# A linear attention and its token normalisation, computed another way in a four-layer hybrid kernel

## The chip, the core and the metric

The kernel runs on one core of one Trainium2 chip. The metric is the time on the device in microseconds (us). Three runs of the kernel before gave 10989.94, 10992.03 and 10992.92 us; the median is 10992.03. One more run was profiled: its span is 10992.0 us.

The core has five engines with a queue each, which run side by side and wait for one another through semaphores: TensorE (PE in the profile, with its weight loads as PEld), VectorE (DVE), ScalarE (ACT), GpSimd (POOL) and SyncE (SP), which issues the DMAs.

## The reference

The input is four images of 64 x 64 tokens with 96 channels. Layers 0 and 1 are selective scans (a state-space layer in four directions); they are not concerned here. Layers 2 and 3 work on the tokens `t`, 4096 per image:

```
t = t + attn(_ln_t(t), Wqkv, bqkv, Wff, bff)
t = t + ffn(_ln_t(t), W1, b1, W2, b2)

_ln_t(v):  (v - mean(v)) / sqrt(var(v) + 1e-5)          over the 96 channels of a token

attn(x):   qkv = x @ Wqkv + bqkv;  q, k, v = split(qkv, 3), 6 heads of 16
           attn = einsum('bhnd,bhmd->bhnm', q, k) * D ** (-0.5)
           y = einsum('bhnm,bhmd->bhnd', attn, v)         # no softmax
           return y @ Wff + bff

ffn(x):    h = relu(_qlinear(x, W1, b1));  return _qlinear(h, W2, b2)
           # _qlinear: inputs and weights rounded to an 8-bit float (5 exponent bits,
           # 2 mantissa bits), results to a 16-bit float
```

There is no softmax, so the two products of the attention can be taken in either order: first `k` transposed times `v`, a 96 x 96 matrix per image, and then the queries times that.

## The kernel before, in words

The scan layers take up the first part of the program. Their results lie in DRAM; four tiles `tok[b]` of 128 x 32 x 96 (partition, token tile, channel) are then loaded, one per image, and stay in SBUF to the end. For each of the layers 2 and 3 the kernel runs `attention` and then `ffn`. Each of the two opens its own pools of tiles and closes them at its end, and loops over the four images.

`token_norm` serves both. Per image it goes over 32 tiles of 128 tokens. On VectorE it takes a statistic (`bn_stats`, L685) and an aggregate (`bn_aggr`, L686) of each tile. `rstd_of` then adds epsilon on VectorE (`tn_ve`, L79) and raises the 128 x 32 variances to the power -0.5 on GpSimd (`tn_rs`, L81). The tiles are normalised into `tn` (L691), three of four on VectorE and the fourth on GpSimd. Groups of four tiles are turned by the PE (L695, channels to the partitions) and evicted by ScalarE (L696), into `tnt` in the attention, and as 8-bit floats into `xq` in the feed-forward.

`attention` then does, per image:

- the queries, 8 products of 512 tokens (L724), evicted by ScalarE into `qt` (L725). `tnt` and `qt` have a 97th row of ones, set by GpSimd (L717, L720), which carries the bias;
- keys and values, 32 products of 128 tokens (L732), evicted in pairs by VectorE into `kv` (L734), and summed over all tokens in `vk` (L736) on the PE;
- `vk` cut to its heads (L745), multiplied with `Wff` (L747) and copied to `wq` (L750), whose last row is the bias `bff`, loaded by DMA for each image (L749);
- the output, 32 products (L755), added to `tok` in groups of four tiles by VectorE (L757).

`ffn` does, per image, 8 chunks of 512 tokens. In each there are three products of 128 hidden channels (L793), cast to a 16-bit float by ScalarE (`h`, L795), bias and relu on VectorE (`hb`, L797), and a cast to an 8-bit float on GpSimd (`hq`, L798). The second product (L802) follows, its eviction on ScalarE (`o`, L806), its bias on VectorE (`ob`, L808) and the addition to `tok` (L810). Layer 3 writes each image out at its end (L812).

The order of the instructions on each engine is laid out when the program is built: an instruction that stands earlier in the program has precedence, and a later one is drawn forward where the layout finds a gap. On the chip each engine takes its queue in that order. Most tiles have two buffers, so the work on the next image can begin while one is under way. The products of 32-bit floats show as two PE records each, the transposes and the 8-bit products as one.

Of the kernel before, what the change touches and what calls it, by code (L numbers as in the profile page):

```python
# [16 lines left out]
F32 = mybir.dt.float32  # L17
# [3 lines left out]
AF = mybir.ActivationFunctionType  # L21
ALU = mybir.AluOpType
# [5 lines left out]
L = HW * HW  # L28
C = 96
# [16 lines left out]
NT = L // 128  # L46
# [29 lines left out]
def rstd_of(nc, pool, var, shape, tag, half):  # L76

    ve = pool.tile(shape, F32, name=f"{tag}_ve")
    nc.vector.tensor_scalar(ve, var, EPS, None, ALU.add)  # L79
    rs = pool.tile(shape, F32, name=f"{tag}_rs")  # L80
    nc.gpsimd.tensor_tensor(rs, ve, half, ALU.pow)  # L81
    return rs
# [594 lines left out]
        finish_sum(len(steps) - 1)  # L677


def token_norm(nc, pool, pp, ident, half, t, out):  # L680

    stats = pool.tile([128, NT, 6], F32, name="tstats")
    mv = pool.tile([128, NT, 2], F32, name="tmv")
    for j in range(NT):
        nc.vector.bn_stats(stats[:, j], t[:, j])  # L685
        nc.vector.bn_aggr(mv[:, j], stats[:, j])  # L686
    rs = rstd_of(nc, pool, mv[:, :, 1], [128, NT], "tn", half)
    tn = pool.tile([128, NT, C], F32, name="tn")
    for j in range(NT):
        eng = nc.gpsimd if j % 4 == 3 else nc.vector  # L690
        eng.tensor_scalar(tn[:, j], t[:, j], mv[:, j, 0:1], rs[:, j : j + 1], ALU.subtract, ALU.mult)  # L691
    for g in range(NT // 4):
        ps = pp.tile([C, 512], F32, name="tnps", tag="tp")
        for j in range(4):
            nc.tensor.transpose(ps[:, 128 * j : 128 * j + 128], tn[:, 4 * g + j], ident)  # L695
        nc.scalar.activation(out[:C, 512 * g : 512 * g + 512], ps, AF.Copy, saturate=False)  # L696


def attention(tc, cst, ident, half, tok, w):

    nc = tc.nc
    with ExitStack() as stage:
        p1 = stage.enter_context(tc.tile_pool(name="t1", bufs=1))
        p2 = stage.enter_context(tc.tile_pool(name="t2", bufs=2))
        pp = stage.enter_context(tc.tile_pool(name="t_ps", bufs=2, space=PSUM))


        wqkv = p1.tile([C + 1, 3 * C], F32, name="wqkv")
        nc.sync.dma_start(out=wqkv[:C], in_=w["Wqkv"])
        nc.sync.dma_start(out=wqkv[C : C + 1], in_=w["bqkv"].unsqueeze(0))  # L710
        wff = p1.tile([C, C], F32, name="wff")
        nc.sync.dma_start(out=wff, in_=w["Wff"])

        for b in range(NB):
            t = tok[b]
            tnt = p2.tile([C + 1, L], F32, name="tnt")
            nc.gpsimd.memset(tnt[C : C + 1], 1.0)  # L717
            token_norm(nc, p2, pp, ident, half, t, tnt)
            qt = p2.tile([C + 1, L], F32, name="qt")
            nc.gpsimd.memset(qt[C : C + 1], 1.0)  # L720
            for c in range(L // 512):
                cols = slice(512 * c, 512 * c + 512)
                ps = pp.tile([C, 512], F32, name="qps", tag="mm")
                nc.tensor.matmul(ps, wqkv[:, :C], tnt[:, cols], start=True, stop=True)  # L724
                nc.scalar.copy(qt[:C, cols], ps)  # L725

            vk = pp.tile([C, C], F32, name="vk", tag="vk", bufs=1)
            for g in range(NT // 2):
                ps = pp.tile([128, 2, 2 * C], F32, name="kvps", tag="mm")
                for j in range(2):  # L730
                    at = 256 * g + 128 * j
                    nc.tensor.matmul(ps[:, j], tnt[:, at : at + 128], wqkv[:, C:], start=True, stop=True)  # L732
                kv = p2.tile([128, 2, 2 * C], F32, name="kv", bufs=3)
                nc.vector.tensor_copy(kv, ps)  # L734
                for j in range(2):
                    nc.tensor.matmul(  # L736
                        vk,
                        kv[:, j, C:],
                        kv[:, j, :C],
                        start=(g == 0 and j == 0),  # L740
                        stop=(g == NT // 2 - 1 and j == 1),
                    )

            heads = p2.tile([C, C], F32, name="heads")
            nc.vector.tensor_tensor(heads, cst["heads"], vk, ALU.mult)  # L745
            ps = pp.tile([C, C], F32, name="wps", tag="vk", bufs=1)
            nc.tensor.matmul(ps, heads, wff, start=True, stop=True)  # L747
            wq = p2.tile([C + 1, C], F32, name="wq")
            nc.sync.dma_start(out=wq[C : C + 1], in_=w["bff"].unsqueeze(0))  # L749
            nc.vector.tensor_copy(wq[:C], ps)  # L750
            for g in range(NT // 4):
                po = pp.tile([128, 4, C], F32, name="ops", tag="o")
                for j in range(4):
                    at = 512 * g + 128 * j
                    nc.tensor.matmul(po[:, j], qt[:, at : at + 128], wq, start=True, stop=True)  # L755
                tg = t[:, 4 * g : 4 * g + 4]
                nc.vector.tensor_tensor(tg, tg, po, ALU.add)  # L757


def ffn(tc, ident, half, tok, w, out=None):  # L760

    nc = tc.nc
    NH = HID // 128
    with ExitStack() as stage:
        p1 = stage.enter_context(tc.tile_pool(name="f1", bufs=1))
        p2 = stage.enter_context(tc.tile_pool(name="f2", bufs=2))
        pp = stage.enter_context(tc.tile_pool(name="f_ps", bufs=2, space=PSUM))
# [15 lines left out]

        for b in range(NB):
            t = tok[b]
            xq = p2.tile([C, L], E5M2, name="xq")
            token_norm(nc, p2, pp, ident, half, t, xq)
            for c in range(L // 512):
                cols = slice(512 * c, 512 * c + 512)
                hq = p2.tile([128, NH, 512], E5M2, name="hq")  # L790
# [25 lines left out]
def hybrid_kernel(ctx: ExitStack, tc: tile.TileContext, a):  # L816
    nc = tc.nc
# [7 lines left out]
    cst = {}  # L825
# [31 lines left out]
    tok = []  # L857
# [1 line left out]
        tok.append(ptok.tile([128, NT, C], F32, name=f"tok{b}"))  # L859
        nc.sync.dma_start(out=tok[b], in_=x[b * L : (b + 1) * L, :].rearrange("(p j) c -> p j c", j=NT))  # L860
    for n in (2, 3):
        attention(tc, cst, ident, half, tok, {k: a[f"l{n}_{k}"] for k in ("Wqkv", "bqkv", "Wff", "bff")})
        ffn(tc, ident, half, tok, {k: a[f"l{n}_{k}"] for k in ("W1", "b1", "W2", "b2")}, a["out"] if n == 3 else None)


# [77 lines left out]
def kernel_arrays(inputs):  # L943
    import numpy as np

    arrays = {"x": np.asarray(inputs["x"]).reshape(NB * L, C), **constants()}
    arrays |= scan_weights(inputs, 0, "out_norm_w") | scan_weights(inputs, 1, "out_norm_g")
    for n in (2, 3):
        for name in ("Wqkv", "bqkv", "Wff", "bff"):
            arrays[f"l{n}_{name}"] = np.asarray(inputs[f"L{n}_attn_{name}"])  # L950
        arrays[f"l{n}_W1"] = np.asarray(inputs[f"L{n}_ffn_W1"]).T
        arrays[f"l{n}_b1"] = np.asarray(inputs[f"L{n}_ffn_b1"]).reshape(HID // 128, 128).T
        arrays[f"l{n}_W2"] = np.asarray(inputs[f"L{n}_ffn_W2"]).T
        arrays[f"l{n}_b2"] = np.asarray(inputs[f"L{n}_ffn_b2"])
    return {name: np.ascontiguousarray(v) for name, v in arrays.items()}
# [16 lines left out]
```

## Time and profile before

| What | us |
|---|---|
| Median of three runs | 10992.03 |
| Span of the profiled run | 10992.0 |
| Scan layers, to the loading of the tokens | 0 to 10262.3 |
| Layer 2, attention | 10262.3 to 10455.5 |
| Layer 2, feed-forward | 10455.5 to 10622.4 |
| Layer 3, attention | 10622.4 to 10818 |
| Layer 3, feed-forward | 10818 to 10992 |

The busy shares over the whole span are PE 75%, VectorE 90%, ScalarE 79% and GpSimd 83%, but most of the span belongs to the scans. A row of the groups gives the line, the engine, the operation, output and inputs by the names of the program, shapes and count; behind the bar stand the busy time and the mean duration of one instruction, and then the idle time of the engine before these instructions with what ended it. A row of the timeline gives the start, the length, the engine, the line and the operation, "xN" for N merged instructions, and in brackets the idle time before it.

### The profile page before, as it was taken

How to read it: one execution, taken by the hardware profiler on the slowest of the kernel's cores; microseconds unless marked ns; L12 is line 12 of the kernel's file. 1: busy time of each engine (PE TensorE's matmuls, PEld its weight loads, DVE VectorE, ACT ScalarE, POOL GpSimd, SP SyncE). 2: the span in 40 equal slices, each digit the busy share in tenths (PEclk: the TensorE clock that was granted, in tenths of full speed). 3: DMA queues.
4: the chain of work that ended last, by engine and by line, in shares of the span. 5: the costliest groups of instructions: out<-in, count | busy, mean ns of one | idle time of the engine just before them, and what ended most of it. 6: DMA issues, size and time to landing. Idle time of an engine off the chain costs nothing. (4 is left out here: it accounts for less than half of the span.)

```text
span 10992.0 us, 145011 instructions
## 1 busy us (share of the span) xinstructions
PE 8224.2 (75%) x48624; PEld 6063.9 (55%) x48624; DVE 9903.3 (90%) x7866; ACT 8663.0 (79%) x18359; POOL 9100.6 (83%) x5250
## 2 busy tenths in 40 slices
PE   7777777777777777777777777776877777776767
PEld 4555555554555555555555555555555555555645
DVE  7999999996999999998899999998899999998576
ACT  6888888885888888885888888886688888887233
POOL 3999999992999999994799999996599999998364
PEclk9889999988889899988888989998888999998767
DMA  4677777774677777776567777777577777777200
GB/s 126 204 206 219 218 220 220 218 213 135 205 212 215 213 218 219 213 218 163 180 208 211 215 218 220 219 214 194 153 206 210 216 219 218 218 216 202 75 3 25
DMA packets 960110, 2114.22 MB, mean 192 GB/s; under 512 B 413154, under 2 KB 704292, under 8 KB 761636
## 3 DMA queue, kind: packets, MB, share of 16 engines
q1 hardware_dynamic: 959364, 2104.94, 66.7%
q8 instruction: 386, 6.32, 0.2%
q14 instruction: 360, 2.95, 0.1%
HBM read 1943.20 MB, written 161.48 MB: 191 GB/s over the span
## 5 line engine op out<-in xcount | busy, mean ns | idle before, releaser
L71 POOL TENSOR_TENSOR h<-h,cb 128x1024 f32<-128x1024 f32 x3072 | 7198.5, 2366 | 271.5 <-issue 83.6
L71 DVE TENSOR_TENSOR_SCAN h<-da,last,bp 128x1024 f32<-128x1024 f32 x2064 | 4735.4, 2335 | 129.7 <-PE bp L71 12.4
L71 ACT ACTIVATE x<-dut,bt 128x128 f32<-128x128 f32 x12288 | 3495.0, 370 | 1.2 <-PE bp L71 0.6
L71 PE MATMUL yp<-ident,h 128*128 128x128 f32 x24576 | 3325.6, 295 | 9.8 <-POOL h L71 9.8
L71 PEld LDWEIGHTS yp<-ident,h 128*128 128x128 f32 x24576 | 3151.7, 155 | 126.9 <-issue 76.3
L71 ACT ACTIVATE da<-delta,amat 128x1024 f32<-128x1024 f32 x2752 | 3063.9, 1138 | 181.9 <-DVE h L71 181.3
L71 PE MATMUL bp<-ident,x 128*128 128x128 f32 x10240 | 1651.6, 313 | 1308.7 <-DVE h L71 902.4
L71 PEld LDWEIGHTS bp<-ident,x 128*128 128x128 f32 x10240 | 1333.6, 160 | 1872.3 <-ACT x L71 1035.2
L71 DVE TENSOR_TENSOR bp<-du,bp 128x1024 f32<-128x1024 f32 x1472 | 1779.8, 1213 | 240.5 <-PE bp L71 238.4
L71 DVE TENSOR_TENSOR_SCAN h<-da,bp 128x1024 f32<-128x1024 f32 x688 | 1537.7, 2274 | 49.2 <-ACT da L71 8.5
L71 PE MATMUL bp<-bparts,sel 96*128 96x512 bf16 x2944 | 929.4, 399 | 845.5 <-DVE h L71 824.4
L71 PEld LDWEIGHTS <-sel 96*128 96x128 bf16 x2944 | 223.8, 100 | 1657.3 <-DVE h L71 1053.9
L71 ACT ACTIVATE bp<-delta,amat 128x1024 f32<-128x1024 f32 x320 | 358.1, 1119 | 541.6 <-DVE h L71 540.4
L71 POOL TENSOR_TENSOR dbu<-du,bb 128x1024 f32<-128x1024 f32 x320 | 754.8, 2359 | 0.0
L71 POOL TENSOR_TENSOR du<-delta,u 128x1024 f32<-128x1024 f32 x192 | 506.6, 2639 | 198.6 <-ACT delta L71 172.9
L81 POOL TENSOR_TENSOR ln_rs<-ln_ve,half 128x4 f32<-128x4 f32 x64 | 83.9, 1311 | 594.1 <-DVE ln_ve L79 493.7
L71 DVE TENSOR_TENSOR_SCAN h<-bp,last,dbu 128x1024 f32<-128x1024 f32 x240 | 558.7, 2328 | 16.4 <-POOL dbu L71 15.3
L71 PE MATMUL xps<-u,wx 128*76 128x512 f32 x768 | 559.9, 818 | 5.7 <-ACT cdt L71 2.9
L71 POOL COPY last<-h 128x2 f32<-128x2 f32 x1152 | 222.0, 193 | 410.1 <-DVE h L71 408.8
L71 ACT ACT_TABLE_LOAD x384 | 492.7, 1283 | 6.8
L71 PE MATMUL dps<-cdt,wdt 12*128 12x512 f32 x768 | 448.2, 664 | 0.1
L71 ACT COPY dut<-dups 128x512 f32<-128x512 f32 x384 | 220.6, 574 | 255.3 <-PE dups L71 255.3
(125 smaller groups left out, 7005.1 us busy)
## 6 DMA issues: line engine op xcount, KB each, us to landing
cb<-crow SPq DMA_DIRECT2D x1024, 1024.0 KB
cb<-crow SPq DMA_DIRECT2D x1024, 512.0 KB
bb<-crow SPq DMA_DIRECT2D x384, 256.0 KB
bb<-crow SPq DMA_DIRECT2D x128, 512.0 KB
y<-ysum SPq DMA_DIRECT2D x192, 256.0 KB
kept<-y SPq DMA_DIRECT2D x160, 256.0 KB
y<-ysum SPq DMA_DIRECT2D x64, 512.0 KB
zt<-zg SPq DMA_DIRECT2D x64, 384.0 KB
```

What stands on the lines that cost most here:

```text
L71: return self.tc.keep_in_program_order(getattr(self.engine, op)(*args, **kwargs))
L81: nc.gpsimd.tensor_tensor(rs, ve, half, ALU.pow)
```

## The change

The keys and values of all tokens are no longer formed. With the normed tokens and a column of ones, `n` = [tn, 1] (4096 x 97), the matrix `n` transposed times `n` (the Gram matrix, 97 x 97) holds all that the sum over the tokens needs: `k` transposed times `v` is Wk-transposed times Gram times Wv, with the biases as the 97th row of the weights. So one accumulation of 32 products per image takes the tiles `tn` as they are, before they are turned. Four small products follow, each evicted by VectorE: Gram with the key weights, the value weights with that, the heads with `Wff`, and the query weights with that. Their result with `bff` added is `whole` (97 x 96), and the turned tokens `tnt` are multiplied with it in the output products. The queries are not formed either. The column of ones is set in `tn` by GpSimd; `qt` and its row of ones are gone.

In `token_norm` the 32 aggregates are gone. `bn_stats` leaves mean and sum of squared deviations of two halves of the channels; five VectorE operations on 128 x 32 values combine them for all 32 tiles at once. The normalisation is scale times token plus shift, with a shift formed on VectorE after the power. Three of four tiles are normalised by ScalarE instead of VectorE, the fourth still by GpSimd. Turning the tokens is a function of its own, `turn_tokens`. The feed-forward uses the same two functions and is otherwise as before.

```diff
-def token_norm(nc, pool, pp, ident, half, t, out):
+def token_norm(nc, pool, half, t, tn):
     stats = pool.tile([128, NT, 6], F32, name="tstats")
-    mv = pool.tile([128, NT, 2], F32, name="tmv")
     for j in range(NT):
         nc.vector.bn_stats(stats[:, j], t[:, j])
-        nc.vector.bn_aggr(mv[:, j], stats[:, j])
-    rs = rstd_of(nc, pool, mv[:, :, 1], [128, NT], "tn", half)
-    tn = pool.tile([128, NT, C], F32, name="tn")
+    (m0, q0), (m1, q1) = ((stats[:, :, i], stats[:, :, i + 1]) for i in (1, 4))
...
+    nc.vector.tensor_tensor(mean2, m0, m1, ALU.add)
+    nc.vector.tensor_tensor(dev, m0, m1, ALU.subtract)
+    nc.vector.scalar_tensor_tensor(dev, dev, 0.25, dev, ALU.mult, ALU.mult)
+    nc.vector.tensor_tensor(var, q0, q1, ALU.add)
+    nc.vector.scalar_tensor_tensor(var, var, 1.0 / C, dev, ALU.mult, ALU.add)
+    rs = rstd_of(nc, pool, var, [128, NT], "tn", half)
+    shift = small("tshift")
+    nc.vector.scalar_tensor_tensor(shift, mean2, -0.5, rs, ALU.mult, ALU.mult)
     for j in range(NT):
-        eng = nc.gpsimd if j % 4 == 3 else nc.vector
-        eng.tensor_scalar(tn[:, j], t[:, j], mv[:, j, 0:1], rs[:, j : j + 1], ALU.subtract, ALU.mult)
+        scale, bias = rs[:, j : j + 1], shift[:, j : j + 1]
+        if j % 4 == 3:
+            nc.gpsimd.tensor_scalar(tn[:, j, :C], t[:, j], scale, bias, ALU.mult, ALU.add)
+        else:
+            nc.scalar.activation(tn[:, j, :C], t[:, j], AF.Identity, bias=bias, scale=scale)
...
+def turn_tokens(nc, pp, ident, tn, out):
...
 def attention(tc, cst, ident, half, tok, w):
...
         for b in range(NB):
             t = tok[b]
+            tn = p2.tile([128, NT, C + 1], F32, name="tn")
+            nc.gpsimd.memset(tn[:, :, C : C + 1], 1.0)
+            token_norm(nc, p2, half, t, tn)
+            gram = pp.tile([C + 1, C + 1], F32, name="gram")
+            for j in range(NT):
+                nc.tensor.matmul(gram, tn[:, j], tn[:, j], start=(j == 0), stop=(j == NT - 1))
             tnt = p2.tile([C + 1, L], F32, name="tnt")
-            nc.gpsimd.memset(tnt[C : C + 1], 1.0)
-            token_norm(nc, p2, pp, ident, half, t, tnt)
-            qt = p2.tile([C + 1, L], F32, name="qt")
-            nc.gpsimd.memset(qt[C : C + 1], 1.0)
-            for c in range(L // 512):
...
-                nc.tensor.matmul(ps, wqkv[:, :C], tnt[:, cols], start=True, stop=True)
-                nc.scalar.copy(qt[:C, cols], ps)
...
-                    nc.tensor.matmul(ps[:, j], tnt[:, at : at + 128], wqkv[:, C:], start=True, stop=True)
-                kv = p2.tile([128, 2, 2 * C], F32, name="kv", bufs=3)
-                nc.vector.tensor_copy(kv, ps)
...
+            turn_tokens(nc, pp, ident, tn, tnt)
+            gk = kept(product(kept(gram, "gram"), wkv[:, :C], "gkps"), "gk")
+            vk = product(wkv[:, C:], gk, "vkps")
             heads = p2.tile([C, C], F32, name="heads")
             nc.vector.tensor_tensor(heads, cst["heads"], vk, ALU.mult)
...
-            nc.sync.dma_start(out=wq[C : C + 1], in_=w["bff"].unsqueeze(0))
-            nc.vector.tensor_copy(wq[:C], ps)
+            rest = kept(product(heads, wff, "hps"), "rest")
+            whole = p2.tile([C + 1, C], F32, name="whole")
+            nc.vector.tensor_tensor(whole, bff, product(wq, rest, "wps"), ALU.add)
             for g in range(NT // 4):
...
-                    nc.tensor.matmul(po[:, j], qt[:, at : at + 128], wq, start=True, stop=True)
+                    nc.tensor.matmul(po[:, j], tnt[:, at : at + 128], whole, start=True, stop=True)
...
 def ffn(tc, ident, half, tok, w, out=None):
...
+            tn = p2.tile([128, NT, C], F32, name="tn")
+            token_norm(nc, p2, half, t, tn)
             xq = p2.tile([C, L], E5M2, name="xq")
-            token_norm(nc, p2, pp, ident, half, t, xq)
+            turn_tokens(nc, pp, ident, tn, xq)
```

Here `product` is one product into a PSUM tile of the tag "small" (two buffers), and `kept` a VectorE copy of it to SBUF. The weights are cut and turned on the host: `wkv` is the key and value part of `Wqkv` with its biases as row 97, `wq` is the query part, turned, with its bias as column 97, and `bff` is a 97 x 96 block of zeros with the bias in its last row.

## The prediction, made before the changed kernel ran

> **What bounds the kernel now.** The page first. VectorE is busy 90% of the span, but the busy shares are those of the selective scans, which end at 10262 us and which the change does not touch. So I went to the stretch behind them, and split it at the instruction that ends each stage (the last update of `tok`): attention, feed-forward, attention, feed-forward.
>
> ```profile
> span 10992.0 us, 145011 instructions
> PE 8224.2 (75%) x48624; PEld 6063.9 (55%) x48624; DVE 9903.3 (90%) x7866; ACT 8663.0 (79%) x18359; POOL 9100.6 (83%) x5250
> ...
> core 0: us, PE busy (x) PEld busy (x) DVE busy (x) ACT busy (x) POOL busy (x), PEclk, DMA share, GB/s
> 10262.30:10455.50 193.20, 156.35 (x968) 130.32 (x968) 117.39 (x461) 36.25 (x64) 72.81 (x44) 0.85 0.06 24
> 10455.50:10622.40 166.90, 97.32 (x608) 54.58 (x608) 139.11 (x523) 83.56 (x160) 118.40 (x132) 0.62 0.01 3
> 10622.40:10818.00 195.60, 157.44 (x968) 132.61 (x968) 117.51 (x462) 36.14 (x64) 72.84 (x44) 0.84 0.01 2
> 10818.00:10992.00 174.00, 98.92 (x608) 55.37 (x608) 138.73 (x522) 83.67 (x160) 118.46 (x132) 0.60 0.10 39
> ```
> The window table gives length, then busy time by engine. The four stages are 193.2, 166.9, 195.6 and 174.0 us, 729.7 in all: nothing that this change does can save more. Nothing overlaps between stages: the first statistic of the feed-forward stands right behind the last update of attention although image 0 had been ready long before. In attention the PE is the longest, 156 of 193 us at a clock of 0.85; in the feed-forward VectorE (139 of 167) and GpSimd (118) share the load and the PE clock is 0.62.
>
> Next the groups inside the first attention stage (line, names, shapes, count | busy, mean ns | idle before):
>
> ```profile
> L732 PE MATMUL kvps<-wqkv,tnt 97*128 97x192 f32 x256 | 57.6, 351 | 0.0
> L734 DVE COPY kv<-kvps 128x384 f32<-128x384 f32 x64 | 35.5, 555 | 35.2 <-PE kvps L732 35.0
> L691 DVE TENSOR_SCALAR tn<-tok,tmv,tn_rs 128x96 f32<-128x96 f32 x96 | 31.2, 453 | 18.3 <-POOL tn_rs L81 18.3
> L81 POOL TENSOR_TENSOR tn_rs<-tn_ve,half 128x32 f32<-128x32 f32 x4 | 21.8, 5446 | 16.2 <-PE kvps L732 11.7 <-DVE tn_ve L79 4.2 <-DVE wq L750 0.2
> ```
> Keys, values and their evictions are the largest part, 57.6 us of PE and 35.5 of VectorE; the power on GpSimd takes 5.4 us, four times. Then the PE in order of time (start, length):
>
> ```profile
> 10355.54 0.84 PE L732 MATMUL kvps<-wqkv,tnt 97*128 97x192 f32 x4
> 10356.22 0.50 PE L736 MATMUL vk<-kv 128*96 128x96 f32 x4
> 10356.56 0.84 PE L732 MATMUL kvps<-wqkv,tnt 97*128 97x192 f32 x4
> 10362.75 0.95 PE L736 MATMUL vk<-kv 128*96 128x96 f32 x4 [5.35 <-DVE kv L734]
> 10363.50 1.54 PE L732 MATMUL kvps<-wqkv,tnt 97*128 97x192 f32 x4
> ...
> 10369.34 0.84 PE L732 MATMUL kvps<-wqkv,tnt 97*128 97x192 f32 x4
> 10370.02 0.50 PE L736 MATMUL vk<-kv 128*96 128x96 f32 x4
> ```
> The PE stood 5.35 us because the eviction of keys and values sat in VectorE's queue behind `tn`, and `tn` behind the power. After it four `vk` records take 0.95 instead of 0.50 us, four `kvps` 1.54 instead of 0.84. So one wait is paid twice, as idle time and as half clock. Last, the seam between two images of the feed-forward, on GpSimd:
>
> ```profile
> 10498.21 1.55 POOL L798 CAST hq<-hb 128x512 fp8e5<-128x512 f16 x2 [0.21 <-DVE hb L797]
> 10504.57 5.46 POOL L81 TENSOR_TENSOR tn_rs<-tn_ve,half 128x32 f32<-128x32 f32 x1 [4.82 <-DVE tn_ve L79]
> 10510.13 5.96 POOL L691 TENSOR_SCALAR tn<-tok,tmv,tn_rs 128x96 f32<-128x96 f32 x8
> 10516.53 0.61 POOL L798 CAST hq<-hb 128x512 fp8e5<-128x512 f16 x1 [0.43 <-PE hps L793]
> ```
> From the last cast of one image to the first of the next GpSimd goes 16.8 us: 4.8 waiting for VectorE's statistics, 5.5 of power, 6.0 of its share of `tn`, 0.4. The cycle is 40.5 us (powers start at 10504.57, 10545.12, 10585.77), 23.8 of it casts.
>
> **What the Trainium skill says.** (1) "TensorE: Matmul & The Clock Gate", Part 1: the array is at half rate until it has been busy for some 3.4 us, and falls back after an idle stretch of that order. The lines above agree (5.35 us idle, then half speed for about 6 us). (2) "ScalarE: Activation LUTs", What ACT_TABLE_LOAD costs: an activation takes 186 ns + 0.833 ns an element, 93 ns more for each pointer operand, and neighbours overlap by 93. The trace has the same form in L289 (192 elements, pointer scale and bias): 533 ns, by the page 532; four of them in 1.86 us, a cadence of 442. No run shows 96 elements, so I take the page's price as an estimate: 452 ns each, 360 ns cadence. (3) "GPSIMD Engine Reference", Key points: GpSimd shares its SBUF interfaces with VectorE. In the trace `tn_ve` took 3.10 us beside a GpSimd memset and 0.17 without one.
>
> **The change part by part.** PE, per image, warm (cadences from the timeline). Before: 32 transposes at 0.109 = 3.5; queries 8 x 0.87 = 7.0; keys and values 32 x 0.34 = 10.9; `vk` 32 x 0.17 = 5.4; output 32 x 0.234 = 7.5; small 0.2; sum 34.5, and the measured warm cycle is 34.4 (outputs start at 10379.25, then 10413.62). After: transposes 3.5, Gram 32 of `vk`'s shape plus one column 5.4, four small products 0.8, output 7.5: 17.2. The 97th column in the transposes and the product is 1%.
>
> VectorE, per image of attention. Gone: 32 aggregations (pairs run at 0.222, a lone statistic at 0.15: 2.3), 24 `tn` (6 to 9), 16 kv evictions (7.5). New: seven operations of 128x32 at about 0.1 (0.7) and four 97-column evictions at 0.25 (1.0). Left: 5.0 + 0.9 + 1.2 + 8 x 0.47 = 10.9.
>
> ScalarE: 8 query evictions go (3.9), 24 `tn` come at 0.36 = 8.6; with 8 turned-token evictions at 0.485 that is 12.5 per image. GpSimd: the two memsets of one partition (3.5 each) go, a memset of 32 columns comes (under 0.2 by the same rate); the power 5.45 and eight `tn` at 0.70 stay: 11.3. That memset waits until the PE has finished the image two before, with the power of its own image behind it; it has a whole image of slack. The new shift waits on VectorE for the power; behind it in that queue stand the token updates of the image before and the next statistics, so a late power holds those up, and through them the PE's two output buffers. DMAs: eight loads of the bias row go, one constant of 97x96 per layer comes, needed 20 us later; nothing, both ways, beside the statistics.
>
> First image: statistics 5.0, combination 0.9, power 5.45, shift 0.2: 11.6; the last ScalarE `tn` at 20.2. The Gram follows at ScalarE's pace even at half clock (four tiles every 1.08 us). Evictions to 24.1, small products beside them (each hop was 0.8 us in the old chain, four hops), outputs to 32. Meanwhile VectorE and GpSimd prepare image 1 (power at about 17 to 22.5), and no queue holds more than 12.5 us per image against 17.2 on the PE. So the stage is the first image's 32, three more at 17.2 = 51.6, the last image's uncovered chain 3.2, the last update 0.6: 87.4. I add 8 for order: the queues are laid out at build time, and the layout takes the power for short (in the seam VectorE has three instructions of the next image between `tn_ve` and `tn`, where the chip then waited 5.3 us), so some instruction will stand in front of ready ones, and the half clock will follow. **95 us against 193: 98 saved per layer.** Bounds: 84 with nothing lost, 138 with no overlap of images.
>
> Feed-forward. ScalarE's pass is longer than VectorE's: from the power's end to the first cast 8.6 + eviction 0.6 + first product and casts 1.4 = 10.6 instead of 6.4; the first cast comes 11.6 + 10.6 = 22.2 us in, instead of 20.9. What this buys is that VectorE is idle in those 8.6 us, so the statistics of the next image (5.9) fit there and the 4.8 us wait goes; the next power can run while ScalarE still normalises. GpSimd's sum decides then: 22.2 + four images of casts 4 x 23.8 + three `tn` shares 3 x 5.6 + two powers 10.9 (the first hides behind ScalarE's pass) + tail 2.5 = 147.6. If the images stay in a row: 22.2 + 95.2 + 3 x (0.3 + 5.45 + 10.6) + 2.5 = 169, 2 more than before. ScalarE's queue carries `tn` of the next image between casts of this one; while it waits for a power, the casts behind it wait too. I add 5 for that: 153. **14 saved per layer.** Chunks of 2.84 us stay: VectorE loses 0.2 us in each, but its operations stretch beside GpSimd's (`hb` 0.335 to 0.69).
>
> Sum: 2 x (98 + 14) = 224; 10992 - 224 = 10768. The profiled span equals the median of the other runs (10992.03), so it is taken as it is.
>
> **Rivals.** (a) Images of attention in a row: each is 20.2 + 3.9 + 0.3 + 7.5 + 0.6 = 32.5, with 2 us of half clock 34.5, so 138, and the feed-forward 169. For it: two tile buffers and in-order queues. Against: the old kernel computed image 1's statistics before image 0's `tn`. Saving 2 x (55 - 2) = 106: 10886. (b) Nothing lost to order: 2 x (107 + 19) = 252: 10740. (c) Attention as forecast, but ScalarE in the feed-forward stands behind each power: three times 8 us on top of 153 gives 177, a loss of 10; 2 x (98 - 10) = 176: 10816. (d) Slower: ScalarE's pass lies fully on the path at price p per tile, no overlap, cold PE. An image of attention is then 11.6 to the shift, 7.4 for the rest of evictions and chain, 15 for cold outputs, 0.6, so 34.6 + 24p against 48.3, one of the feed-forward changes by 24p - 8.6 against now. Over eight of each they break even at p = 0.47; at p = 0.533 (L289's whole duration, its neighbours not overlapping) it is 7 less and 33 more: 11018. Against: L289's cadence. That less is computed than stated is no rival: the diff drops lines 724 and 732 outright.
>
> **How the numbers follow.** Forecast 0.50; (b) 0.16; (c) 0.16; (a) 0.13; (d) 0.05, of which 0.03 beyond the bound. Within 0.2% (22 us, what a measurement of this kernel can tell) 0.02. The forecast's own range is 10745 to 10795; (b) carries the low end to 10715 (147 and 84 with cheaper chunks), (c) and most of (a) the high end to 10880.
>
> **What would show it.** Attention stages of 90 to 100 us, PE over 75% busy there with a clock above 0.9; `tn` on ScalarE at 450 ns; powers of image b+1 before the outputs of image b; in the feed-forward no wait for `tn_ve`, and powers under 37 us apart. Wrong if the PE idles over 3 us per image, or if ScalarE's groups name the power as the releaser for tens of us.

## The result, and the profile after

The changed kernel takes 10827.67 us (median of four runs, 10820.52 to 10831.02) against 10990.99 for the kernel before: a ratio of 0.9852, with a 95% interval of 0.9835 to 0.9869. It is faster by 163 us; 224 had been forecast. The time lies in the range given (10715 to 10880), but outside the forecast's own range (10745 to 10795).

From the page of the changed kernel, the lines that answer to those of before: span, and busy time by engine over the whole span.

```profile
span 10818.7 us, 143079 instructions
PE 8073.8 (75%) x48032; PEld 5963.0 (55%) x48032; DVE 9699.3 (90%) x6962; ACT 8758.7 (81%) x18679; POOL 9001.7 (83%) x5242
```

The shares hardly moved, since the scans fill them. The stages are read from the window table of the changed kernel, cut again at the last update of `tok` in each stage (window, length, busy time by engine, the share of its full clock that the PE was granted, DMA share):

```profile
core 0: us, PE busy (x) PEld busy (x) DVE busy (x) ACT busy (x) POOL busy (x), PEclk, DMA share, GB/s
10252.90:10360.40 107.50, 83.56 (x672) 81.76 (x672) 46.74 (x208) 51.74 (x128) 35.10 (x40) 0.79 0.10 43
10360.40:10532.80 172.40, 100.27 (x608) 55.23 (x608) 110.22 (x323) 116.48 (x256) 106.47 (x132) 0.61 0.01 3
10532.80:10640.20 107.40, 82.52 (x672) 80.67 (x672) 47.30 (x210) 51.73 (x128) 35.08 (x40) 0.80 0.01 3
10640.20:10818.70 178.50, 100.55 (x608) 56.26 (x608) 110.52 (x322) 116.40 (x256) 106.59 (x132) 0.60 0.09 38
```
Each attention stage fell from 193 and 196 to 107 us, and each feed-forward stage rose by 4 to 6 us. The token part went from 729.7 to 565.8: 163.9 us, the whole difference of the medians. The scan part, whose code is the same everywhere, ended between 10249 and 10267 us in the profiled runs of all the kernels below, so these are read by their token stages. Where two kernels share the code of a stage, its time agrees within 0.9 us (attention 86.0, 86.4 and 86.1 in experiments 4, 7 and 9).

**Attention.** The groups of the first attention stage:

```profile
L769 PE MATMUL ops<-whole,tnt 97*128 97x96 f32 x256 | 38.3, 313 | 3.9 <-DVE whole L764 3.9
L705 ACT ACTIVATE tn<-tok,tshift,tn_rs 128x96 f32<-128x96 f32 x96 | 35.8, 457 | 21.5 <-DVE tshift L699 21.5
L754 PE MATMUL gram<-tn 128*97 128x97 f32 x256 | 32.0, 279 | 16.6 <-ACT tn L705 16.6
L81 POOL TENSOR_TENSOR tn_rs<-tn_ve,half 128x32 f32<-128x32 f32 x4 | 21.7, 5430 | 27.4 <-DVE tn_ve L79 27.4
```
The largest groups of before, `kvps` (57.6 us) and the `kv` evictions (35.5), are gone, and `gram` with 32.0 is new. But `ops` still takes 38.3 us for 256 records, where the warm ones come at 0.122 each (31.2). The reason is in the first image. PE in order of time, changed kernel:

```profile
10280.18 0.64 PE L739 MATMUL gkps<-wkv,gram 97*97 97x96 f32 x2 [4.91 <-DVE gram L744]
...
10289.95 3.73 PE L769 MATMUL ops<-whole,tnt 97*128 97x96 f32 x16 [3.90 <-DVE whole L764]
...
10318.50 2.02 PE L769 MATMUL ops<-whole,tnt 97*128 97x96 f32 x16
```
Two waits for VectorE, and after them 16 records take 3.73 us instead of 2.02. VectorE at the same time:

```profile
10276.10 0.19 DVE L699 SCALAR_TENSOR_TENSOR tshift<-tmean,tn_rs 128x32 f32<-128x32 f32 x1 [5.22 <-POOL tn_rs L81]
10276.21 3.76 DVE L684 BATCH_NORM_STATS2 tstats<-tok 128x6 f32<-128x96 f32 x23
10279.89 0.24 DVE L744 COPY gram<-gram 97x97 f32<-97x97 f32 x1
...
10288.58 0.19 DVE L699 SCALAR_TENSOR_TENSOR tshift<-tmean,tn_rs 128x32 f32<-128x32 f32 x1 [4.79 <-POOL tn_rs L81]
10288.69 1.05 DVE L684 BATCH_NORM_STATS2 tstats<-tok 128x6 f32<-128x96 f32 x6
10289.66 0.24 DVE L764 TENSOR_TENSOR whole<-bff,wps 97x96 f32<-97x96 f32 x1
```
The short evictions of image 0 (`gram`, `whole`) stand behind `tshift` of images 1 and 2. `tshift` waits for the 5.4 us of the power, and all that is behind it in VectorE's queue waits with it: first the statistics (3.76 and 1.05 us here), then the eviction. It is the wait of the kernel before, with another instruction in front.

**Feed-forward.** GpSimd at the start of the stage (which begins at 10360.4), from its timeline:

```profile
10368.78 5.43 POOL L81 TENSOR_TENSOR tn_rs<-tn_ve,half 128x32 f32<-128x32 f32 x1 [47.38 <-DVE tn_ve L79]
10379.97 5.43 POOL L81 TENSOR_TENSOR tn_rs<-tn_ve,half 128x32 f32<-128x32 f32 x1 [2.20 <-DVE tn_ve L79]
10391.23 5.43 POOL L81 TENSOR_TENSOR tn_rs<-tn_ve,half 128x32 f32<-128x32 f32 x1 [2.27 <-DVE tn_ve L79]
10398.49 0.61 POOL L814 CAST hq<-hb 128x512 fp8e5<-128x512 f16 x1 [1.83 <-DVE hb L813]
```
Three powers, for images 0, 1 and 2, run before the first cast of image 0. ScalarE and VectorE show why that cast was late:

```profile
10388.06 0.57 ACT L811 CAST h<-hps 128x512 f16<-128x512 f32 x1
...
10396.69 0.19 DVE L699 SCALAR_TENSOR_TENSOR tshift<-tmean,tn_rs 128x32 f32<-128x32 f32 x1 [5.29 <-POOL tn_rs L81]
10396.80 1.37 DVE L684 BATCH_NORM_STATS2 tstats<-tok 128x6 f32<-128x96 f32 x8
10398.09 0.34 DVE L813 TENSOR_SCALAR hb<-h,b 128x512 f16<-128x512 f16 x1
```
Its input `h` was ready at 10388.63, but the first `hb` of image 0 stands behind `tshift` of image 2. So the first cast comes 38.1 us into the stage, against 20.9 before. From one image's first cast to the next it is then 37.3, 35.5 and 36.6 us instead of 40.1 to 40.6. Together: 17.2 lost at the start, 11.9 won on three periods, a few tenths lost behind them, 5.5 lost in all. One thing still stands at the seam between two images, on ScalarE (here ahead of image 2's first cast on GpSimd at 10471.30):

```profile
10458.54 0.48 ACT L822 CAST o<-ops 128x384 f16<-128x384 f32 x1 [0.26 <-PE ops L818]
10458.92 1.54 ACT L705 ACTIVATE tn<-tok,tshift,tn_rs 128x96 f32<-128x96 f32 x4
10461.38 0.48 ACT L822 CAST o<-ops 128x384 f16<-128x384 f32 x1 [0.93 <-PE ops L818]
10461.76 5.12 ACT L705 ACTIVATE tn<-tok,tshift,tn_rs 128x96 f32<-128x96 f32 x14
```
Of the 24 tiles of the next image 23 are normalised after the last cast of `h` (at 10457.70), 18 of them in these two stretches, although ScalarE idles some 0.8 us in each of the 2.84 us chunks.

### The profile page after: what moved, and what is told of

Its sections match the earlier page's. It is cut to its first block, busy times and chain, and to the rows that moved or that the text cites. A ratio compares the mean times of both kernels' runs of the same rounds, so it can differ in the third digit from the quotient of the medians.

```text
span 10818.7 us, 143079 instructions
## 1 busy us (share of the span) xinstructions
PE 8073.8 (75%) x48032; PEld 5963.0 (55%) x48032; DVE 9699.3 (90%) x6962; ACT 8758.7 (81%) x18679; POOL 9001.7 (83%) x5242
## 5 line engine op out<-in xcount | busy, mean ns | idle before, releaser
L71 POOL TENSOR_TENSOR h<-h,cb 128x1024 f32<-128x1024 f32 x3072 | 7198.4, 2367 | 268.9 <-issue 77.4
L71 DVE TENSOR_TENSOR_SCAN h<-da,last,bp 128x1024 f32<-128x1024 f32 x2064 | 4735.9, 2335 | 132.2 <-PE bp L71 15.1
L71 ACT ACTIVATE x<-dut,bt 128x128 f32<-128x128 f32 x12288 | 3495.3, 370 | 0.8 <-PE bp L71 0.5
L71 PE MATMUL yp<-ident,h 128*128 128x128 f32 x24576 | 3324.6, 295 | 9.8 <-POOL h L71 9.8
L71 PEld LDWEIGHTS yp<-ident,h 128*128 128x128 f32 x24576 | 3151.3, 155 | 126.4 <-issue 75.4
L71 ACT ACTIVATE da<-delta,amat 128x1024 f32<-128x1024 f32 x2752 | 3063.9, 1138 | 173.1 <-DVE h L71 172.9
L71 PE MATMUL bp<-ident,x 128*128 128x128 f32 x10240 | 1652.4, 312 | 1319.9 <-DVE h L71 920.8
L71 PEld LDWEIGHTS bp<-ident,x 128*128 128x128 f32 x10240 | 1333.4, 160 | 1880.0 <-ACT x L71 1046.2
L71 DVE TENSOR_TENSOR bp<-du,bp 128x1024 f32<-128x1024 f32 x1472 | 1779.2, 1213 | 230.3 <-PE bp L71 228.2
L71 DVE TENSOR_TENSOR_SCAN h<-da,bp 128x1024 f32<-128x1024 f32 x688 | 1537.7, 2274 | 48.8 <-ACT da L71 8.1
L71 PE MATMUL bp<-bparts,sel 96*128 96x512 bf16 x2944 | 922.5, 396 | 831.4 <-DVE h L71 810.4
L71 PEld LDWEIGHTS <-sel 96*128 96x128 bf16 x2944 | 224.3, 100 | 1640.5 <-DVE h L71 1030.3
L71 ACT ACTIVATE bp<-delta,amat 128x1024 f32<-128x1024 f32 x320 | 358.1, 1119 | 536.9 <-DVE h L71 535.5
L71 POOL TENSOR_TENSOR dbu<-du,bb 128x1024 f32<-128x1024 f32 x320 | 754.9, 2359 | 0.0
L71 POOL TENSOR_TENSOR du<-delta,u 128x1024 f32<-128x1024 f32 x192 | 506.8, 2640 | 202.3 <-ACT delta L71 176.5
L71 DVE TENSOR_TENSOR_SCAN h<-bp,last,dbu 128x1024 f32<-128x1024 f32 x240 | 558.7, 2328 | 16.8 <-POOL dbu L71 13.1
L71 PE MATMUL xps<-u,wx 128*76 128x512 f32 x768 | 561.0, 820 | 5.7 <-ACT cdt L71 2.9
L71 POOL COPY last<-h 128x2 f32<-128x2 f32 x1152 | 223.0, 194 | 396.3 <-DVE h L71 394.4
L71 PE MATMUL dps<-cdt,wdt 12*128 12x512 f32 x768 | 448.0, 664 | 0.1
L71 ACT COPY dut<-dups 128x512 f32<-128x512 f32 x384 | 220.9, 575 | 255.0 <-PE dups L71 255.0
```

The lines of the kernel that those rows point to most:

```text
L71: return self.tc.keep_in_program_order(getattr(self.engine, op)(*args, **kwargs))
```

## The experiments

The stages of every kernel that ran, in us (layer 2, then layer 3), and for the feed-forward of layer 2 the first cast on GpSimd from the start of the stage, the three periods from one image's first cast to the next, and the rest. Ratios are to the runs of the kernel before in the same batch.

| Kernel | attention | feed-forward | first cast, periods, rest | median | ratio (95% interval) |
|---|---|---|---|---|---|
| before | 193.2, 195.6 | 166.9, 174.0 | 20.9; 40.1 40.5 40.6; 24.9 | 10990.99 | |
| changed | 107.5, 107.4 | 172.4, 178.5 | 38.1; 37.3 35.5 36.6; 25.3 | 10827.67 | 0.9852 (0.9835 to 0.9869) |
| 1 Gram alone | 116.0, 116.1 | 167.2, 173.4 | 21.1; 39.9 39.9 40.3; 26.0 | 10828.23 | 0.9853 (0.9839 to 0.9868) |
| 2 normalisation alone | 172.9, 172.7 | 172.2, 178.1 | 37.4; 37.2 35.6 36.8; 25.1 | 10954.45 | 0.9970 (0.9958 to 0.9981) |
| 3 power left out | 81.9, 80.8 | 157.1, 164.0 | 22.5; 35.8 37.0 36.6; 25.2 | 10740.89 | 0.9773 (0.9758 to 0.9788) |
| 4 shift on GpSimd | 86.0, 85.9 | 166.9, 172.9 | 32.4; 37.3 35.6 36.4; 25.1 | 10770.13 | 0.9798 (0.9781 to 0.9814) |
| 5 VectorE tiles in feed-forward | 107.7, 107.5 | 163.0, 168.3 | 19.7; 39.2 39.7 38.6; 25.9 | 10811.93 | 0.9837 (0.9820 to 0.9853) |
| 6 square root | 83.1, 82.5 | 157.0, 162.6 | 22.9; 36.7 36.6 35.6; 25.0 | 10753.48 | 0.9785 (0.9771 to 0.9800) |
| 7 first order by hand | 86.4, 86.8 | 223.4, 229.3 | 37.1; 53.3 54.1 53.4; 25.6 | 10886.54 | 0.9908 (0.9893 to 0.9923) |
| 8 the same with square root | 83.0, 82.4 | 207.8, 213.8 | 32.4; 49.2 50.5 50.5; 25.2 | 10853.88 | 0.9876 (0.9861 to 0.9891) |
| 9 second order, power | 86.1, 86.7 | 152.5, 158.4 | 22.2; 35.5 34.1 32.9; 27.8 | 10746.86 | 0.9780 (0.9764 to 0.9796) |
| 10 second order, square root | 83.6, 82.6 | 139.1, 144.7 | 17.5; 32.9 31.3 29.6; 27.8 | 10711.84 | 0.9747 (0.9732 to 0.9761) |
| 11 the same, a tile to VectorE | 83.0, 81.9 | 141.3, 146.9 | 16.4; 35.2 33.2 30.1; 26.6 | 10714.34 | 0.9748 (0.9733 to 0.9762) |

**1 and 2: the two halves of the change.** In 1 the attention is the changed kernel's and `token_norm` does the arithmetic of before, writing into `tn`; in 2 the attention is that of before with the new `token_norm`.

```diff
# 1, in the changed kernel
-    ... five operations that combine the statistics, tshift
-            nc.scalar.activation(tn[:, j, :C], t[:, j], AF.Identity, bias=bias, scale=scale)
+        nc.vector.bn_aggr(mv[:, j], stats[:, j])
...
+        eng = nc.gpsimd if j % 4 == 3 else nc.vector
+        eng.tensor_scalar(tn[:, j, :C], t[:, j], mv[:, j, 0:1], rs[:, j : j + 1], ALU.subtract, ALU.mult)
```

> Only the Gram form of the attention; the token normalisation is the old one (32 aggregates, three of four tiles on VectorE), so the feed-forward stage is the one of before. Theory (the gain is the PE's work that is gone, the loss in the feed-forward is the new normalisation): attention stages fall from 193 to about 120 us, since VectorE now has 21 us per image (statistics and aggregates 7, tiles 9, the rest 5) against 17 on the PE; feed-forward stays at 167 and 174. Sum: 10991 - 2 x 74 = about 10845, so within 20 us of the changed kernel. Rival (the normalisation on ScalarE carries half of the attention's gain): attention stays above 145 and the time above 10890.

> Only the new token normalisation (combined statistics, three of four tiles on ScalarE) with the old attention of queries, keys and values. Theory: the PE keeps its 34.4 us per image, so attention falls only by what its waits cost, to about 170 us; the feed-forward is that of the changed kernel, 172 and 178 us, 5 longer than before. Sum: 10991 - 2 x 23 + 10 = about 10955. Rival (the normalisation carries half of the attention's gain): attention at 150 or less, 10910.

Both came out near their first theories. The Gram matrix alone gives 77 to 80 us per attention stage and leaves the feed-forward as it was, and its total is that of the changed kernel. The normalisation alone gives 20 to 23 us in attention and costs 4 to 5 in the feed-forward. On top of the Gram matrix it gives only 8.6 in attention, and the 5 of the feed-forward take more than half of it back. So nearly the whole gain is the Gram matrix.

**3: is it the wait of `tshift` for the power?** The power becomes a product of the same shape on the same engine. This leaves the power out of the computation; order and count of the instructions on every queue of the token stages stay.

```diff
-    rs = rstd_of(nc, pool, var, [128, NT], "tn", half)     # its last operation: ALU.pow
+    ve = small("tn_ve")
+    nc.vector.tensor_scalar(ve, var, EPS, None, ALU.add)
+    rs = small("tn_rs")
+    nc.gpsimd.tensor_tensor(rs, ve, half, ALU.mult)
```

> The changed kernel with the power of the token norms left out: GpSimd multiplies the same 128x32 tiles instead, so the tokens are scaled by another number. The order of all queues is that of the changed kernel, instruction by instruction. Theory 1 (VectorE's shift waits for the power of a later image, and the casts and the small products' evictions stand behind it): attention falls from 107.5 to about 87 us (5.2 of the first power, 8.8 of PE idle behind the evictions, some 6 of half clock), the feed-forward from 172.4 to about 155 (5.2 of the first power, 9.5 of the first hb behind the third shift, 2 at the next seam). Sum: 10828 - 2 x 38 = 10752. Theory 2 (ScalarE's pass of 24 tiles sets the start and the seams by itself): only the first power of a stage counts, 5 us per stage, 10808.

In the groups of the two stages (attention first, then feed-forward) the operation shrinks from 5430 to 250 ns:

```profile
L697 POOL TENSOR_TENSOR tn_rs<-tn_ve,half 128x32 f32<-128x32 f32 x4 | 1.0, 251 | 19.2 <-DVE tn_ve L695 19.2
L699 DVE SCALAR_TENSOR_TENSOR tshift<-tmean,tn_rs 128x32 f32<-128x32 f32 x4 | 0.8, 193 | 0.5 <-POOL tn_rs L697 0.4
```
```profile
L699 DVE SCALAR_TENSOR_TENSOR tshift<-tmean,tn_rs 128x32 f32<-128x32 f32 x4 | 0.8, 193 | 3.8 <-POOL tn_rs L697 3.5
```
VectorE's idle time at `tshift` in the feed-forward falls from 24.5 us to 3.8. Attention falls by 26 us and the feed-forward by 15, near what Theory 1 had. All of the latter is at the first cast (38.1 to 22.5); the periods stay at 36.5. So in this order the power's length hurts where an image has nothing in front of it, and not in the run of the chunks.

**4: the wait moved, the power kept.** `tshift` goes to GpSimd, behind the power that it needs; -0.5 is multiplied in earlier, on VectorE.

```diff
+    nc.vector.tensor_scalar(mean2, mean2, -0.5, None, ALU.mult)
     rs = rstd_of(nc, pool, var, [128, NT], "tn", half)
-    nc.vector.scalar_tensor_tensor(shift, mean2, -0.5, rs, ALU.mult, ALU.mult)
+    nc.gpsimd.tensor_tensor(shift, mean2, rs, ALU.mult)
```

> The changed kernel with the shift formed on GpSimd, right behind the power, from a mean that VectorE has scaled before; VectorE waits for no power any more. The layout of the queues may change with it. Theory 1: in attention the evictions of the small products no longer stand behind a power, PE idle of 4.9 and 3.9 us and part of the half clock go, 107.5 becomes 92 to 98; in the feed-forward the first cast of GpSimd still stands behind the third power in GpSimd's own queue, so 172.4 becomes 168 to 171. Sum: about 10828 - 2 x 14 = 10800. Theory 2 (ScalarE's pass): no change beyond 3 us per stage.

It is better than I had expected: 86.0 us in attention, 21.5 less than the changed kernel, with every power still there. PE in this kernel, image 0 (stage start 10260.7):

```profile
10283.07 0.41 PE L739 MATMUL gkps<-wkv,gram 97*97 97x96 f32 x2
10287.03 1.92 PE L769 MATMUL ops<-whole,tnt 97*128 97x96 f32 x16
10288.96 1.95 PE L769 MATMUL ops<-whole,tnt 97*128 97x96 f32 x16
```
No wait ahead of them, warm from the first, 26.3 us into the stage instead of 37.1. Both experiments agree. The layout shifts a little in this one, while in experiment 3 it is that of the changed kernel; and what is left between the two, 81.9 and 86.0, lies ahead of the first outputs (22.1 and 26.3 us in), where the first image still needs its power. In the feed-forward only 5.5 us come back: VectorE is free, but GpSimd itself still has the powers of images 0, 1 and 2 ahead of the first cast (starts 8.5, 17.6 and 26.7 us in, first cast at 32.4).

**5 and 6: what holds the feed-forward.** In 5 its three of four tiles go back to VectorE; in 6 the power is a square root on ScalarE and a reciprocal on VectorE. Both start from the changed kernel.

```diff
# 5
-            nc.scalar.activation(tn[:, j, :C], t[:, j], AF.Identity, bias=bias, scale=scale)
+            if three == "vector":                  # given by ffn alone
+                nc.vector.tensor_scalar(tn[:, j, :C], t[:, j], scale, bias, ALU.mult, ALU.add)
+            else:
+                nc.scalar.activation(tn[:, j, :C], t[:, j], AF.Identity, bias=bias, scale=scale)
# 6
-    rs = rstd_of(nc, pool, var, [128, NT], "tn", half)
+    ve, rs = small("tn_ve"), small("tn_rs")
+    nc.vector.tensor_scalar(ve, var, EPS, None, ALU.add)
+    nc.scalar.activation(ve, ve, AF.Sqrt)
+    nc.vector.reciprocal(rs, ve)
```

> The changed kernel, but in the feed-forward stages the three of four tiles are normalised on VectorE again, with the combined statistics kept. It asks which part of the new normalisation costs the feed-forward its 5 us. Theory A (ScalarE's 24 tiles per image stand behind the last cast of h, so the seam between two images grows): the stage goes from 172.6 and 178.6 back to 166-169 and 172-175, the median to about 10816, and the waits of ScalarE's h for hb at a seam shrink from 11-12.5 us to under 9. Rival B (tshift, waiting in VectorE's queue for the power, holds the first hb and the seams whoever writes the tiles): the stage stays at 172-178, since tshift is still there and 24 tiles of 0.25 us are added to VectorE's queue behind it. Attention stays at 107-108.

> The changed kernel with the power on GpSimd (5.43 us for 128x32) replaced by a square root on ScalarE and a reciprocal on VectorE; all else as in the changed kernel, tshift stays on VectorE. Theory A (the 5.43 us of the power, waited for in VectorE's queue, is what attention and the feed-forward lost): attention 82-87 (with the power left out it was 81-82), feed-forward 157-161, median 10740-10760. Rival B (ScalarE loads its table again for each square root, 16 times at something above 1 us, and the square root stands in ScalarE's queue between the evictions): attention above 92, feed-forward above 165, median above 10785.

5 refutes both of its theories. The stage falls to 163.0, below theory A's 166 to 169, but not for A's reason: the periods are longer (39.2 against 36.5), and from the end of image 0's last cast to the first of image 1 GpSimd goes 15.0 us, against 12.0 in the changed kernel. ScalarE's tiles are thus a gain of 2.7 us per image in the steady run. What 5 wins is the start. GpSimd in this kernel (stage start 10371.2):

```profile
10378.95 5.43 POOL L81 TENSOR_TENSOR tn_rs<-tn_ve,half 128x32 f32<-128x32 f32 x1 [46.84 <-DVE tn_ve L79]
10384.71 3.81 POOL L703 TENSOR_SCALAR tn<-tok,tn_rs,tshift 128x96 f32<-128x96 f32 x8 [0.33 <-DVE tshift L699]
10390.87 0.61 POOL L817 CAST hq<-hb 128x512 fp8e5<-128x512 f16 x1 [2.36 <-DVE hb L816]
```
One power, then the first cast, 19.7 us in. With tiles of its own VectorE goes from them to `hb`. In the changed kernel it is free while ScalarE normalises, and in the gap the layout drew forward the statistics and shifts of images 1 and 2. That this freedom is why the layout differs is my reading; that the order differs, and costs 18 us, is measured.

6 does what theory A said: 83.1 and 157.0, and the first cast at 22.9. The one table load that the square root brings shows up once:

```profile
10267.15 1.28 ACT L699 ACT_TABLE_LOAD   x1 [14.10 <-DVE tn_ve L698]
10268.44 0.23 ACT L699 ACTIVATE tn_ve<-tn_ve 128x32 f32<-128x32 f32 x1
```
After it ScalarE goes on between the square root, the tiles and the evictions without another. "ScalarE: Activation LUTs" of the Trainium skill, in its part on table sets, says that loads come by set and not by function, and the trace agrees.

**7 to 11: the order of the feed-forward written out.** In 7 (on top of 4) and 8 (on top of 6) each engine keeps the order of the program, and statistics, tiles and turns of image b+1 stand between the chunks of image b.

> The kernel with tshift on GpSimd (10770, feed-forward 166.9 and 172.9), and in the feed-forward stages the order of every engine written out by hand: statistics, power, tiles and turning of image b+1 are placed between the chunks of image b, a few tiles per chunk, and each chunk's second product stands behind the next chunk's first. Theory A (the seams of 11-12.5 us are a matter of order: ScalarE's tiles stand behind the last cast, while ScalarE has idle time inside the chunks): in the feed-forward window of that kernel the sums per image are ScalarE 31 us, VectorE 30.5, GpSimd 27; with about 22 us until the first cast, three images at 31, one at 23 and 5 us of drain the stage is 143-153, the median 10720-10745. Rival B (GpSimd is the bound: its casts, powers and tiles come to 27 us an image and each power of 5.43 us stops the chunks wherever it stands): periods stay at 35-36 us and the stage at 163 or more.

> Both: square root and reciprocal instead of the power, tshift on VectorE, and the feed-forward's order by hand. If the power and the order are two separate losses, attention is that of the square root alone (82-87) and the feed-forward 135-147, median 10695-10720. If the order by hand gives nothing beyond a shorter power, the feed-forward stays at 155-160 and the median at that of the square root alone.

Both failed: the stage grew to 223 and 208 us. In the sketch, "turn" and "keep" are the four transposes and their eviction, and `i` counts chunks over all images:

```diff
# 7 and 8, per chunk i
+ h(i), hb(i), hq(i); tiles(g); turn(g); keep(g) for one or two groups g; second product of i-1
# 9, 10 and 11
+ h(i), hb(i), hq(i); keep(i+1); second product of i-1; turn(i+2); tiles(i+3); 4 statistics of the next image
```
One chunk of 7, from its timeline (all lines are those of the helper, L71):

```profile
10467.30 1.48 PE L71 MATMUL hps<-xq,w1q 96*128 96x512 fp8e5 x3
...
10467.97 1.56 ACT L71 CAST h<-hps 128x512 f16<-128x512 f32 x3
...
10469.40 1.19 ACT L71 ACTIVATE tn<-tok,tshift,tn_rs 128x96 f32<-128x96 f32 x3
...
10469.94 1.16 PE L71 MATMUL tnps<-ident,tn 128*96 128x128 f32 x3 [1.16 <-ACT tn L71]
...
10472.33 0.59 ACT L71 ACTIVATE xq<-tnps 96x512 fp8e5<-96x512 f32 x1 [1.74 <-PE tnps L71]
```
Casts, tiles, turns and eviction follow one another, each on the other engine's result, and the second product, which had been ready, stands behind the turns. An order by hand can be right in which image it serves and still wrong within one chunk. The second order leaves a chunk between any two of these.

> A second order by hand for the feed-forward, after the first one made each chunk a chain: its trace shows ScalarE's three tiles, the four turns, the second product, its eviction and then the next chunk's casts one after another, 5.7 us a chunk with one group of tiles and 8.2 with two, against 2.84 before. Here nothing of a chunk waits for work of the same chunk: at chunk i stand the casts of h of i, the eviction of the turns of i+1, the second product of i-1, the turns of i+2 and the tiles of i+3, and the statistics of the next image run four tiles a chunk. Power and tshift on GpSimd, as in the kernel of 10770. If the seams are order alone: ScalarE needs 3 x 0.52 + 0.59 + 0.48 + 1.18 = 3.8 us a chunk, so 12 + 32 x 3.95 + 2 = 140, plus up to 5 us for each of three powers in GpSimd's queue: 142-155, median 10720-10750. If the chunks stay tied to each other by waits, 165 or more.

> The same order with the square root on ScalarE and the reciprocal on VectorE in place of the power. If the order is right and ScalarE sets the chunk: 136-146 against 156.9 with the square root alone, median 10710-10735; the difference to the kernel with the power is what the power still costs when nothing but GpSimd's casts stands behind it. If the seam was not what held the square root's kernel, the stage stays at 155 or more.

> The same as the last, but one of the three ScalarE tiles of a group goes to VectorE: ScalarE 3.45 us a chunk, VectorE about 3.5. If ScalarE's 0.39 us per tile is on the path of the ordered feed-forward: 125-137, 8-12 us less than the last, median 10690-10715. If VectorE or GpSimd is as near, no less than 3 us change.

9 and 10 came out as expected, 152.5 and 139.1 us. Between them lie power or square root and reciprocal, with the place of `tshift`, and 13.4 us: 4.7 at the first cast and 8.7 on the three periods. In 10 the first cast comes at 17.5 and the periods are 29.6 to 32.9. 11 missed its 125 to 137: no gain, 2 us worse, which is its other branch, that another engine is as near. VectorE in 10, in order of time, shows which:

```profile
10401.75 1.23 DVE L71 TENSOR_SCALAR hb<-h,b 128x512 f16<-128x512 f16 x3
10402.90 0.96 DVE L71 TENSOR_TENSOR ob<-o,b 128x384 f16<-128x384 f16 x1
10403.90 0.85 DVE L71 TENSOR_TENSOR tok<-tok,ob 128x384 f32<-128x384 f32 x1
10404.67 0.73 DVE L71 BATCH_NORM_STATS2 tstats<-tok 128x6 f32<-128x96 f32 x4
10405.32 1.22 DVE L71 TENSOR_SCALAR hb<-h,b 128x512 f16<-128x512 f16 x3
```
There is no gap in this chunk, and VectorE sets it, 10405.32 - 10401.75 = 3.57 us. A tile more on it (0.32 us in the trace of 11) makes the chunk longer, 3.79 us by the starts of `tn` there (10402.52, 10406.31). The sum of 3.5 for VectorE was too small; `ob` and `tok` take 0.96 and 0.85 here, where a chunk of 7 shows 0.56 for each.

10 is the fastest kernel that ran: 277 us below the kernel before in the medians of its own batch, where the changed kernel was 163 below.

## Why the prediction was right or wrong

**Right: the mechanism of attention, and its warm rate.** Outputs of images 1, 2 and 3 start at 10318.50, 10335.55 and 10351.29: 17.1 us for an image beside the next one's Gram matrix, where 17.2 was worked out, and 15.7 for the step to the last. ScalarE's tile took 457 ns in this trace for the estimate of 452 from the Trainium skill's page "ScalarE: Activation LUTs", and 24 of them 8.7 us for 8.6. The four token stages account for the whole difference.

**Mis-sized: attention's first image.** The term was 87.4 plus 8 for order and half clock. By its own parts: first outputs at 24.5, measured 37.1; from there to the next image's outputs 17.2, measured 28.6; two more at 17.2, measured 17.1 and 15.7; an end of 11.3, measured 9.1. The sum is 107.5, so the allowance should have been 20. The prediction had named the place: "the new shift waits on VectorE for the power", with statistics and token updates behind it. What it left out of that list are the five short evictions of the Gram chain. A queue's list must hold what the change itself puts on it. Without that wait, in experiment 4, the stage is 86.0 against the sum of 87.4, in part because its errors cancel: first outputs at 26.3, then 17.9, 17.1 and 15.7, and an end of 9.1.

**Wrong: the feed-forward's gain of 14.** Two terms of the sum failed. The first cast, taken at 22.2 us, came at 38.1, since the sum assumed that image 0 has the queues to itself: its shift came at 13.8 for 11.6, and from there to the cast it took 24.3 for 10.6. With the power's length left out (experiment 3) that stretch is 13.9, so 10.4 of the 15.9 us are the powers of images 1 and 2. And the periods: casts 23.8, tiles 5.6 and two thirds of 5.45 us of power make 33.0 per image, measured 36.5. GpSimd's own tiles were cheaper (8 at 0.43 are 3.4), but ScalarE's stood after the last cast of an image, not inside its chunks: in two of the three seams GpSimd waited 11.0 and 12.5 us and did nothing else. Added up, 15.9 + 10.4 lost, 1 won at the end, and the allowance of 5 used: 153 becomes 173. The sum of 147.6 was a bound of GpSimd, and the layout did not reach it; experiment 9, with the same power on GpSimd but the order by hand, runs in 152.5.

**Luck.** That the time still lies in the range owes something to chance. Its high end was there for images in a row and for ScalarE behind each power, and neither happened; two other losses, 10 to 12 us in each attention stage and 18 to 20 in each feed-forward, came to 61 us and stayed inside.

**The rivals.** (c) lay nearest in time (10816), but with attention as forecast, which it was not. Its idea, a queue standing behind each power, is the right one, on VectorE and at the first image, not on ScalarE three times a stage. (b) is what experiment 4 shows for attention. (d) had its price decided: the tile's cadence is 0.36 us, below its break-even of 0.47. (a) did not happen: images overlap from the second on.

**The signs named beforehand.** The PE was to be busy over 75% in attention with a clock above 0.9: 83.56 of 107.5 is 78%, but at 0.79, with the half clock of image 0 in it (0.90 in experiment 4). Powers of image b+1 before the outputs of b: yes, and VectorE's wait for them did the harm. Powers in the feed-forward under 37 us apart: no, they are 11.2, 11.3 and 38.5 apart, three in a bunch. No wait for `tn_ve`: nearly, two of 2.2 us at the start instead of 4.8 at a seam. "Wrong if the PE idles over 3 us per image": 4.9 and 3.9 us on image 0, none later. ScalarE naming the power for tens of us: its groups name `tshift`, 21.5 us in attention and 22.5 in the feed-forward, but 20.1 and 21.0 of these lie ahead of image 0's first tile, and part of that even before the stage.

## What to carry to other kernels

It can pay to put a short instruction that waits for a long one on the engine of the long one. `tshift`, 0.19 us of work on VectorE, held that queue for the power's 5 us, and moving it to GpSimd was worth 57 us, as much as a third of the whole change. Most of that is attention; in the feed-forward, where GpSimd's own casts stand behind its powers, it gave back 5.5 us a stage. When work is moved off an engine, ask what the layout will draw into the gap, and whether this waits: the freed time went to images 1 and 2 while image 0 stood behind them. And a sum per engine is a bound on the rate; first instance and order have to be priced by themselves.

## What the runs showed of the hardware that I had not expected

A GpSimd tile of 128 x 96 takes 0.42 us in the changed kernel and took 0.74 in the kernel before. The rows for `tn` in the attention of the two (minimum, median, maximum in ns), before and then changed:

```profile
L691 POOL TENSOR_SCALAR tn<-tok,tmv,tn_rs x32: 680/740/801, 10282.2 to 10366.7; 128x96 f32<-128x96 f32 x32
```
```profile
L703 POOL TENSOR_SCALAR tn<-tok,tn_rs,tshift x32: 415/422/425, 10265.2 to 10321.0; 128x96 f32<-128x96 f32 x32
```
The operation is nearly the same (subtract and multiply, now multiply and add), so one would look at the neighbours. But the difference stays where VectorE stands still. Three tiles of the kernel before, in the middle one of which VectorE has no work (from 10330.95 to 10332.12), then six of the changed kernel, most of them without any beside them (from 10438.16 to 10440.89):

```profile
10330.71 2.05 POOL L691 TENSOR_SCALAR tn<-tok,tmv,tn_rs 128x96 f32<-128x96 f32 x3
10332.12 0.56 DVE L757 TENSOR_TENSOR tok<-tok,ops 128x384 f32<-128x384 f32 x1 [1.17 <-PE ops L755]
```
```profile
10437.71 2.59 POOL L703 TENSOR_SCALAR tn<-tok,tn_rs,tshift 128x96 f32<-128x96 f32 x6
10440.89 0.67 DVE L813 TENSOR_SCALAR hb<-h,b 128x512 f16<-128x512 f16 x1 [2.73 <-POOL hq L814]
```
That is 0.68 us a tile against 0.43. So most of the gain goes with the form of the operation; whether it is the subtraction or the other layout of the mean, no run separates. The prediction had kept 0.70.

The neighbour adds to it. "GPSIMD Engine Reference" of the Trainium skill says, under Key points, that the two engines contend when VectorE runs in a two-port mode or reads two inputs from SBUF. It fits in part. The old form takes 0.76 where VectorE normalises beside it (the kernel before and experiment 1). The new form takes 0.42 beside statistics and 0.71 in experiment 10 beside `ob` and `tok`, which have two inputs and are drawn out themselves (0.96 and 0.85 us). Beside VectorE's own tiles in experiment 5 it takes only 0.44 to 0.51. `bn_stats` is not drawn out by a GpSimd tile: in the changed kernel its median is 0.24 us with a tile beside it and without.
